# One power for both norms of a mixing layer, its squares summed on the scalar engine, and its plain rows written later

## The chip, the core and the metric

The kernel runs on one core of a Trainium2 chip. A core has five engines that each work through a queue of their own, in order, and wait for each other by semaphores: TensorE (PE, matrix products and transposes; PEld is its weight load), VectorE (DVE), ScalarE (ACT), GpSimd (POOL, which also issues the gathers), and SyncE (SP, which here only issues plain DMAs). The metric is the device time of one execution in microseconds (us), the median of a few runs.

## The reference

The input is eight sequences (batches) of 512 rows with 128 features. Six layers follow one another, each added to the rows: a mixture of experts, attention, the same experts again, a layer whose operands are rounded to six bits (fp6), the mixing layer with a gated feed-forward, and the fp6 layer once more. The change lies in the fifth. With x the normalised input of that layer, n its layer norm:

```python
def _layernorm(x): return (x - mean(x)) / sqrt(var(x) + 1e-5)
def _rmsnorm(x, w): return x * rsqrt(mean(x * x) + 1e-6) * w

n = _layernorm(x)                       # the rows that the layer takes
xn = _rmsnorm(n, rms_mix_w)
g, v, d = xn @ Wg.T + bg, xn @ Wv.T + bv, xn @ Wd.T + bd
h = scan(h * (0.001 + 0.998 * sigmoid(d)) + sigmoid(g) * tanh(v))   # along the sequence
u = n + h
xf = _rmsnorm(u, rms_ffn_w)
y = u + (silu(xf @ W_gate.T) * (xf @ W_up.T)) @ W_out.T
x = x + y
```

The layer therefore needs two norms of the same input, n and xn, then a third of u. All norms go over the 128 features of a row.

## The kernel before, in words

A batch is held in SBUF as `X[b]`, 128 partitions by 4 tiles of 128 features, so a row lies in one partition and a batch's statistics are 128 by 4 numbers. Everything stays in SBUF from the first layer to the last, except the rows that are sorted to experts through DRAM.

**Tails.** The last three layers of a batch, from the first fp6 layer to the store, are its tail: `tail(b)` runs `fp6(b, 3)`, `mix(b)`, `fp6(b, 5)` and then issues the store on SP. A tail starts when both experts' outputs of its batch have been gathered (POOL's indirect DMAs, tile `y`) and added (`x<-y,g,x` on DVE). Eight tails run, and at most four at a time: `flight = Slots(4)` in line 1392. A tail that finds no slot waits until another has stored. Smaller counters do the same for parts: `rounding`, `turning`, `gating` and `feeding`, two each (line 1275).

**Order.** The instruction order on each engine is that of the program (`tc.manual_schedule()`), and the program's order is made by a planner, the class `Clock`. Each tail is a Python generator; a `yield` ends one step. `finish` takes the generator that is ready first by the planner's own rough costs (`took`) and lets it issue its next step on whatever engines that step names. So a `yield` is a place where steps of other tails, of the experts' tiles or of a gather can come between; without it, the instructions stand back to back in their queues. Because a queue is in order, an instruction that waits also holds back everything behind it, whoever's it is.

**The norms.** `moments` makes mean and variance by bn_stats and bn_aggr on DVE. `power` (line 401) adds an epsilon on DVE and raises to -1/2 on POOL, 128 by 4 numbers. `normed_act` (line 419) makes the shift -mean/sigma on DVE and then scales and shifts the four tiles on ACT, with scale and bias read per partition.

**mix before.** Its first part is a chain over the engines: moments (DVE, tiles `st_m`, `mv_m`), epsilon (DVE) and power (POOL, `rs_m`), two products that give the mean square of n (DVE, `r`), the shift (DVE, `nb_um_m`), the plain rows u (ACT, `um_m`), a second epsilon (DVE) and power (POOL) in `rs_ma`, its product with `rs_m` (DVE), a second shift (DVE, `nb_row_m`), and the rows xn (ACT, `row_m`). Then PE transposes xn (`tp_xn`), ACT copies it out with the weight (`uT_xn`), PE makes three products (`pgd`, `pgg`, `pgv`), and ACT takes their tanh (`gtd`, `gtg`, `gtv`). DVE maps the decay to 0.499 d + 0.5 (`gtd`), makes the scan's input (`gtg`) and scans (`scan`), PE turns the result back (`tp_h`), and DVE adds it to u (`um_m<-tp_h,um_m`).

Its second part is the feed-forward. Moments of u (DVE, `st_f`, `mv_f`), mean squared plus variance (two on DVE, `r2f`), epsilon (DVE) and power (POOL, `rs_mb`), `X[b] + u` (POOL), u scaled (ACT, `xf`), transposed and copied, six products (`gt`, `up`), silu on ACT and a product on DVE for each of three pairs, twelve products into `yo`, and the addition to X.

Tiles come from pools with a fixed number of buffers per tag: `um` has 4 (u of the mixing layer and of the fp6 layers), and `row` has 4 (xn, the scan's output, xf).

Of the kernel before, what the change touches and what calls it, by code (L numbers as in the profile page):

```python
# [9 lines left out]
F32 = mybir.dt.float32  # L10
BF16 = mybir.dt.bfloat16
I32 = mybir.dt.int32
AF = mybir.ActivationFunctionType
ALU = mybir.AluOpType
# [3 lines left out]
P = 128  # L18
S = 512
NT = S // P  # L20
# [214 lines left out]
def kernel(  # L235
# [18 lines left out]
    ck = Clock(nc)  # L254
    nb = x.shape[1] // S
    assert nb == 8
    scale = 1.0 / float(DK) ** 0.5
# [3 lines left out]
    wk = ctx.enter_context(tc.tile_pool(name="wk", bufs=2))  # L261
    small = ctx.enter_context(tc.tile_pool(name="small", bufs=5))
# [5 lines left out]
    X = []  # L268
# [29 lines left out]
    mhalf = cpool.tile([P, GTX], F32, tag="mhalf", name="mhalf")  # L298
# [87 lines left out]
    def bank(name):  # L386
        return p_ps.tile([P, S], F32, tag="ps", name=name)
# [5 lines left out]
    def turned(src, name):  # L393

        tp = bank(f"tp_{name}")
        for t in range(NT):
            ck.tensor.transpose(tp[:, ts(t, P)], src[:, t, :], ident)
        return tp


    def power(v, eps, name):
        rs = small.tile([P, NT], F32, tag="rs", name=f"rs_{name}")
        ck.vector.tensor_scalar_add(rs, v, eps)
        yield
        ck.gpsimd.tensor_tensor(rs, rs, mhalf[:, 0:NT], ALU.pow)
        yield
        return rs

    def moments(src, name, mv=None):
        st = small.tile([P, NT, ck.vector.BN_STATS_DIM], F32, tag="bst", name=f"st_{name}")  # L410
        if mv is None:
            mv = small.tile([P, NT, ck.vector.BN_AGGR_DIM], F32, tag="bmv", name=f"mv_{name}")
        for t in range(NT):
            ck.vector.bn_stats(out=st[:, t, :], in_=src[:, t, :])
        for t in range(NT):
            ck.vector.bn_aggr(out=mv[:, t, :], in_=st[:, t, :])
        return mv

    def normed_act(src, mv, rs, name, tag="u"):

        nb_ = small.tile([P, NT], F32, tag="nbias", name=f"nb_{tag}_{name}")
        ck.vector.scalar_tensor_tensor(nb_, mv[:, :, 0], -1.0, rs, ALU.mult, ALU.mult)
        yield
        u = wk.tile([P, NT, P], F32, tag=tag, name=f"{tag}_{name}", bufs={"um": 4, "row": 4}.get(tag, 2))
        for t in range(NT):
            ck.scalar.activation(
                u[:, t, :], src[:, t, :], AF.Identity,
                scale=rs[:, t : t + 1], bias=nb_[:, t : t + 1],
            )
        yield "product"  # L430
        return u
# [11 lines left out]
    def by_feature(src, name, scale=None, tag="uT"):  # L443

        tp = turned(src, name)
        yield
        ut = wk.tile([P, S], F32, tag=tag, name=f"uT_{name}")
        if scale is None:
            ck.scalar.copy(ut, tp)
        else:  # L450
            ck.scalar.activation(ut, tp, AF.Copy, scale=scale)
        yield "product"
        return ut
# [850 lines left out]
    def vec(i):  # L1304
        return vec_s[:, i : i + 1]

    def mix(b):
        mv = moments(X[b], f"m_{b}")
        rs = yield from power(mv[:, :, 1], 1e-5, f"m_{b}")

        r2 = small.tile([P, NT], F32, tag="r2", name=f"r2_{b}")
        ck.vector.tensor_tensor(r2, rs, rs, ALU.mult)
        ck.vector.tensor_tensor(r2, r2, mv[:, :, 1], ALU.mult)
        u = yield from normed_act(X[b], mv, rs, f"m_{b}", tag="um")
        rr = yield from power(r2, 1e-6, f"ma_{b}")
        ck.vector.tensor_tensor(rr, rr, rs, ALU.mult)
        xn = yield from normed_act(X[b], mv, rr, f"m_{b}", tag="row")
        yield from turning.take()
        xnt = yield from by_feature(xn, f"xn_{b}", scale=vec(V_MIX))
        yield from gating.take()  # L1320

        def gate(i, bias, half, n):
            pg = bank(f"pg{n}_{b}")
            ck.tensor.matmul(pg, wmix_s[:, ts(i, P)], xnt, start=True, stop=True)
            t = wk.tile([P, S], F32, tag=("qm", "ka", "qa")[i], name=f"gt{n}_{b}", bufs=(2, KBUFS, 2)[i])
            ck.scalar.activation(t, pg, AF.Tanh, bias=bias, scale=half)
            return t


        d = gate(2, half_vec[:, 1:2], 0.5, "d")  # L1330
        g = gate(0, half_vec[:, 0:1], 0.5, "g")
        vv = gate(1, vec(V_BV), 1.0, "v")
        turning.give()
        yield
        ck.vector.tensor_scalar(d, d, 0.499, 0.5, ALU.mult, ALU.add)
        ck.vector.scalar_tensor_tensor(g, g, 1.0, vv, ALU.add, ALU.mult)
        h = wk.tile([P, NT, P], F32, tag="row", name=f"scan_{b}", bufs=4)
        ck.vector.tensor_tensor_scan(
            h.rearrange("p t d -> p (t d)"), d, g, 0.0, ALU.mult, ALU.add
        )  # L1340
        gating.give()
        yield
        ht = turned(h, f"h_{b}")
        yield
        uf = u.rearrange("p t d -> p (t d)")
        ck.vector.scalar_tensor_tensor(uf, ht, 0.5, uf, ALU.mult, ALU.add)
        mv = moments(u, f"f_{b}")
        r2 = small.tile([P, NT], F32, tag="r2", name=f"r2f_{b}")
        ck.vector.tensor_tensor(r2, mv[:, :, 0], mv[:, :, 0], ALU.mult)
        ck.vector.tensor_tensor(r2, r2, mv[:, :, 1], ALU.add)  # L1350
        rr = yield from power(r2, 1e-6, f"mb_{b}")
        ck.gpsimd.tensor_tensor(X[b], X[b], u, ALU.add)
        xf = wk.tile([P, NT, P], F32, tag="row", name=f"xf_{b}", bufs=4)
        for t in range(NT):
            ck.scalar.activation(xf[:, t, :], u[:, t, :], AF.Copy, scale=rr[:, t : t + 1])
        yield
        yield from feeding.take()
        xft = yield from by_feature(xf, f"xf_{b}", scale=vec(V_FFN), tag="u")
        yield from gating.take()
        sgs = []  # L1360
        for f in range(NGF):
            pg, pu = bank(f"gt_{b}_{f}"), bank(f"up_{b}_{f}")
            ck.tensor.matmul(pg, wmix_s[:, ts(3 + f, P)], xft, start=True, stop=True)
            ck.tensor.matmul(pu, wmix_s[:, ts(6 + f, P)], xft, start=True, stop=True)
            sg = wk.tile([P, S], F32, tag=("qm", "ka", "qa")[f], name=f"silu_{b}_{f}", bufs=(2, KBUFS, 2)[f])
            ck.scalar.activation(sg, pg, AF.Silu)
            yield
            ck.vector.tensor_tensor(sg, sg, pu, ALU.mult)
            sgs.append(sg)
            yield  # L1370
        yo = bank(f"yo_{b}")
        for t in range(NT):
            for f in range(NGF):
                ck.tensor.matmul(
                    yo[:, ts(t, P)], sgs[f][:, ts(t, P)], wout_s[:, f, :],
                    start=(f == 0), stop=(f == NGF - 1),
                )
        gating.give()
        feeding.give()
        yield  # L1380
        xb = X[b].rearrange("p t d -> p (t d)")
        ck.vector.tensor_tensor(xb, xb, yo, ALU.add)

    def tail(b):
        yield from fp6(b, 3)
        yield from mix(b)
        yield from fp6(b, 5)
        nc.sync.dma_start(
            out=out[:, ts(b, S)].rearrange("p (t d) -> p t d", t=NT), in_=X[b]
        )  # L1390
# [130 lines left out]
```

## Time and profile before

| | |
|---|---|
| median of 3 runs | 1151.93 us (1150.66 to 1154.56) |
| the profiled execution, its own time | 1150.87 us |
| its span, first to last instruction | 1149.2 us |
| mean granted TensorE clock | 0.923 |
| busy over the span | PE 960.0, DVE 706.1, POOL 544.8, ACT 483.4 us |
| instructions | 20659 |
| first and last start of a tail's first bn_stats (tile `st`, late part) | 844 us, 1055.20 us |

All instructions show line 185, that of a helper which records every operation for the planner, so they are told apart by tile names. Times inside a row of the timeline are counted from the start of the span. A row's name is output<-inputs, with numbers of buffers and batches left out. In a list of waits, "A <- B" is idle time of A's engine that ended with B. A table of groups gives how often an instruction ran, its total and its mean duration. Many short DVE operations overlap a little with their neighbours, so a sum of durations is slightly more than the time that they fill.

### The profile page before, as it was taken

The numbers are of one execution on the slowest core, as the hardware profiler recorded it, in microseconds if no ns is written. First come the engines' busy times: TensorE is split into PE (matmuls) and PEld (weight loads), VectorE is DVE, ScalarE is ACT, GpSimd is POOL, SyncE is SP. The second block draws the span as 40 slices with busy tenths as digits, with TensorE's granted clock in tenths as the row PEclk, the third lists the DMA queues.
The fourth block names the chain that finished last, engine by engine and source line by source line (L and its number), as shares of the span: only waits on it lengthen the run. The fifth ranks groups of instructions, "written<-read, shape, count | busy, mean of one in ns | idle before, by whom it ended". The sixth has DMA issues, their size and how long they took to land.

```text
span 1149.2 us, 20659 instructions
## 1 busy us (share of the span) xinstructions
PE 960.0 (84%) x6705; PEld 662.2 (58%) x6705; DVE 706.1 (61%) x2636; ACT 483.4 (42%) x1063; POOL 544.8 (47%) x694
## 2 busy tenths in 40 slices
PE   3569999999998989999997999998089985765773
PEld 2469999776444444444545767767077764433542
DVE  7323345466878877767795655314256786888764
ACT  1323333325554545455554544543034544344531
POOL 3777071213876845454552231231745646864422
PEclk9999999999998988989999999999589998887786
DMA  9579788756900100000014444342366401100000
GB/s 294 192 248 277 234 263 255 212 177 173 284 22 26 32 12 8 13 9 13 8 33 140 123 136 121 118 141 61 116 201 189 142 20 37 31 25 10 1 19 18
DMA packets 122363, 127.33 MB, mean 111 GB/s; under 512 B 9616, under 2 KB 103696, under 8 KB 122256
## 3 DMA queue, kind: packets, MB, share of 16 engines
q1 hardware_dynamic: 114064, 109.22, 31.5%
q0 software_dynamic: 8192, 16.79, 4.6%
q8 instruction: 53, 0.87, 0.3%
q14 instruction: 54, 0.44, 0.1%
HBM read 79.58 MB, written 46.40 MB: 110 GB/s over the span
## 4 chain that ended last, share of the span: by engine, by line
PE 63%; DVE 19%; POOL 6%; issue 5%; ACT 3%; DMA 2%; SPq 1%; POOLq 0%; DVEq 0%; ACTq 0%
PE yp L185 14%; PE hp L185 14%; PE sa L185 10%; PE av L185 6%; PE sb L185 4%; DVE seen L185 2%; DVE q L185 2%; DVE x L185 2%; POOL y L185 2%; PE xp L185 2%; DVE st L185 1%; PE lp L185 1%; PE yo L185 1%; ACT um L185 1%; PE tp L185 1%
## 5 line engine op out<-in xcount | busy, mean ns | idle before, releaser
L185 DVE CUSTOM_DVE_ANT_0 seen<-sa,future_s 128x128 f32<-128x128 f32 (+3 forms) x512 | 224.7, 487 | 92.5 <-PE sb L185 74.9
L185 ACT ACTIVATE pm<-sb 128x512 f32<-128x512 f32 (+1 forms) x384 | 182.1, 524 | 201.0 <-PE sb L185 188.0
L185 ACT ACTIVATE hs<-hp,wx 128x256 f32<-128x256 f32 x276 | 120.6, 471 | 265.7 <-PE hp L185 236.5
L185 PE MATMUL sb<-qa,ka 32*128 32x512 f32 (+3 forms) x1024 | 224.4, 480 | 8.8 <-DVE nstat L185 6.8
L185 POOL TENSOR_SCALAR_AFFINE_SELECT pm<-pm 128x256 f32<-128x256 f32 x256 | 101.1, 409 | 223.0 <-ACT pm L185 219.9
L185 PE MATMUL sa<-ka,qz 32*128 32x256 f32 (+3 forms) x1024 | 200.6, 477 | 1.6 <-issue 1.6
L185 PE MATMUL yp<-wx,hs 128*128 128x128 f32 x1472 | 198.7, 278 | 2.5 <-DVE hs L185 2.0
L185 PE MATMUL hp<-xt,wx 128*128 128x256 f32 x736 | 198.6, 395 | 0.0
L185 PEld LDWEIGHTS yp<-wx,hs 128*128 128x128 f32 x1472 | 188.8, 194 | 13.0 <-issue 5.2
L185 POOL DMA_INDIRECT y<-rows_out,at x128 | 136.1, 1064 | 85.6 <-DMA rows_out<-yo 41.8
L185 DVE TENSOR_SCALAR hs<-hp,wx 128x256 f32<-128x256 f32 x92 | 44.3, 481 | 175.6 <-ACT hs L185 157.1
L185 PEld LDWEIGHTS hp<-xt,wx 128*128 128x128 f32 x736 | 131.4, 197 | 27.3 <-issue 10.2
L185 PEld LDWEIGHTS sa<-ka,qz 32*128 32x128 f32 x1024 | 96.6, 190 | 61.8 <-issue 19.6
L185 PEld LDWEIGHTS sb<-qa,ka 32*128 32x128 f32 x1024 | 106.0, 189 | 26.8 <-DVE nstat L185 14.2
L185 PE MATMUL av<-pm,vpad 128*32 128x512 f32 (+3 forms) x1024 | 92.1, 455 | 0.0
L185 POOL TENSOR_TENSOR rs<-rs,mhalf 128x4 f32<-128x4 f32 (+1 forms) x36 | 39.7, 1104 | 97.6 <-DVE rs L185 94.7
L185 PE MATMUL xp<-cst,xs 128*128 128x128 f32 x184 | 37.9, 290 | 51.7 <-DMA xs<-by_stretch 38.4
L185 POOL DMA_INDIRECT by_stretch<-um,sat x64 | 64.4, 1007 | 18.5 <-issue 14.4
L185 PEld LDWEIGHTS xp<-cst,xs 128*128 128x128 f32 x184 | 26.4, 149 | 63.2 <-issue 51.5
L185 PEld LDWEIGHTS av<-pm,vpad 128*32 128x32 f32 x1024 | 23.6, 109 | 66.2 <-issue 42.3
L185 DVE COPY xt<-xp 128x256 f32<-128x256 f32 x92 | 38.2, 415 | 37.3 <-PE xp L185 37.2
L185 DVE SCALAR_TENSOR_TENSOR x<-y,g,x 128x128 f32<-128x128 f32 x128 | 55.8, 439 | 3.6 <-DMA y<-rows_out,at 1.3
(219 smaller groups left out, 1332.8 us busy)
## 6 DMA issues: line engine op xcount, KB each, us to landing
wx<-in_wexp SPq DMA_DIRECT2D x92, 578.0 KB, 4.0
rows_out<-yo SPq DMA_DIRECT2D x92, 128.0 KB, 1.8
by_stretch<-zero SPq DMA_DIRECT2D x8, 1280.0 KB
rows_in<-zero SPq DMA_DIRECT2D x2, 3456.0 KB
by_stretch<-zero SPq DMA_DIRECT2D x8, 768.0 KB, 11.9
xs<-rows_in SPq DMA_DIRECT2D x46, 128.0 KB, 4.4
xs<-by_stretch SPq DMA_DIRECT2D x46, 128.0 KB, 3.4
x<-in_x SPq DMA_DIRECT2D x8, 256.0 KB, 5.4
```

Source lines behind the costliest of these rows:

```text
L185: return call(*args, **kw)
```

## The change

In `mix` both powers are taken together. Since the mean square of n is v/(v + 1e-5) for variance v, the second norm's factor is the power -1/2 of v(1 + 1e-6) + 1e-6 * 1e-5. One tile `rs2` of 128 by 2 by 4 gets both arguments (two DVE operations), one POOL power and one DVE operation for both shifts (`nb2`). The rows xn are made directly after; the plain rows u are made on ACT after the gates. The map of the decay to 0.499 d + 0.5 goes from DVE to ACT. In the feed-forward the moments of u and the two operations on them go; ACT squares the four tiles of u with a sum along the row into `r2` (its output is the buffer of xf, which is written over afterwards), and one DVE operation scales by 1/128 and adds the epsilon. Further `yield`s stand between these steps. No DMA, no matrix product and no buffer count changes.

```diff
     def mix(b):
         mv = moments(X[b], f"m_{b}")
-        rs = yield from power(mv[:, :, 1], 1e-5, f"m_{b}")
-
-        r2 = small.tile([P, NT], F32, tag="r2", name=f"r2_{b}")
-        ck.vector.tensor_tensor(r2, rs, rs, ALU.mult)
-        ck.vector.tensor_tensor(r2, r2, mv[:, :, 1], ALU.mult)
-        u = yield from normed_act(X[b], mv, rs, f"m_{b}", tag="um")
-        rr = yield from power(r2, 1e-6, f"ma_{b}")
-        ck.vector.tensor_tensor(rr, rr, rs, ALU.mult)
-        xn = yield from normed_act(X[b], mv, rr, f"m_{b}", tag="row")
+        rs2 = small.tile([P, 2, NT], F32, tag="rs2", name=f"rs2_{b}")
+        ck.vector.tensor_scalar(
+            rs2[:, 1], mv[:, :, 1], 1.0 + 1e-6, 1e-6 * 1e-5, ALU.mult, ALU.add
+        )
+        ck.vector.tensor_scalar_add(rs2[:, 0], mv[:, :, 1], 1e-5)
+        yield
+        ck.gpsimd.tensor_tensor(
+            rs2, rs2, mhalf[:, 0 : 2 * NT].rearrange("p (k t) -> p k t", k=2), ALU.pow
+        )
+        yield
+        nb2 = small.tile([P, 2, NT], F32, tag="nb2", name=f"nb2_{b}")
+        ck.vector.scalar_tensor_tensor(
+            nb2, mv[:, :, 0].unsqueeze(1).to_broadcast([P, 2, NT]), -1.0, rs2, ALU.mult, ALU.mult
+        )
+        yield
+        xn = wk.tile([P, NT, P], F32, tag="row", name=f"xn_{b}", bufs=4)
+        u = wk.tile([P, NT, P], F32, tag="um", name=f"um_m_{b}", bufs=4)
+
+        def scaled(dst, k, lo, hi):
+            for t in range(lo, hi):
+                ck.scalar.activation(
+                    dst[:, t, :], X[b][:, t, :], AF.Identity,
+                    scale=rs2[:, k, t : t + 1], bias=nb2[:, k, t : t + 1],
+                )
+
+        scaled(xn, 1, 0, NT)
+        yield "product"
         yield from turning.take()
         xnt = yield from by_feature(xn, f"xn_{b}", scale=vec(V_MIX))
         yield from gating.take()
...
         g = gate(0, half_vec[:, 0:1], 0.5, "g")
         vv = gate(1, vec(V_BV), 1.0, "v")
         turning.give()
-        yield
-        ck.vector.tensor_scalar(d, d, 0.499, 0.5, ALU.mult, ALU.add)
+        ck.scalar.activation(d, d, AF.Copy, scale=0.499, bias=0.5)
+        scaled(u, 0, 0, NT)
+        yield
         ck.vector.scalar_tensor_tensor(g, g, 1.0, vv, ALU.add, ALU.mult)
...
         ck.vector.scalar_tensor_tensor(uf, ht, 0.5, uf, ALU.mult, ALU.add)
-        mv = moments(u, f"f_{b}")
+        yield
+
+        xf = wk.tile([P, NT, P], F32, tag="row", name=f"xf_{b}", bufs=4)
         r2 = small.tile([P, NT], F32, tag="r2", name=f"r2f_{b}")
-        ck.vector.tensor_tensor(r2, mv[:, :, 0], mv[:, :, 0], ALU.mult)
-        ck.vector.tensor_tensor(r2, r2, mv[:, :, 1], ALU.add)
-        rr = yield from power(r2, 1e-6, f"mb_{b}")
+        for t in range(NT):
+            ck.scalar.activation(
+                xf[:, t, :], u[:, t, :], AF.Square, accum_out=r2[:, t : t + 1]
+            )
+        yield
+        rr = small.tile([P, NT], F32, tag="rs", name=f"rs_mb_{b}")
+        ck.vector.tensor_scalar(rr, r2, 1.0 / P, 1e-6, ALU.mult, ALU.add)
+        yield
+        ck.gpsimd.tensor_tensor(rr, rr, mhalf[:, 0:NT], ALU.pow)
         ck.gpsimd.tensor_tensor(X[b], X[b], u, ALU.add)
-        xf = wk.tile([P, NT, P], F32, tag="row", name=f"xf_{b}", bufs=4)
+        yield
         for t in range(NT):
             ck.scalar.activation(xf[:, t, :], u[:, t, :], AF.Copy, scale=rr[:, t : t + 1])
         yield
```

## The prediction

> **What bounds the kernel now.** I read the busy time by stage first, then the engines' timelines over the last stage, then the list of waits there, and last the groups of instructions for durations. Times are us from the start of the span. First, busy time of each engine in three stretches: the first tails beside the last expert tiles, then the second set of gathers, then the end.
>
> ```profile
> core 0: us, PE busy (x) PEld busy (x) DVE busy (x) ACT busy (x) POOL busy (x), PEclk, DMA share, GB/s
> 845.00:960.00 115.00, 101.68 (x591) 83.51 (x590) 82.61 (x258) 56.50 (x126) 60.98 (x55) 0.96 0.39 118
> 960.00:1055.00 95.00, 57.05 (x222) 36.62 (x221) 76.35 (x225) 39.71 (x88) 67.32 (x61) 0.77 0.09 25
> 1055.00:1149.00 94.00, 61.76 (x255) 41.99 (x253) 61.24 (x180) 34.97 (x76) 32.72 (x30) 0.78 0.04 14
> ```
>
> See in the last two rows that no engine is full: DVE is at 80% and 65%, PE at 60% and 66%, ACT at 42% and 37%. Everything changed lies after 844, where the tails begin, so the 844 us before are untouched. What sets the end after 960 is latency, the time that one tail needs from engine to engine, with DVE's queue as the main delay. Next, DVE's timeline where the last tail starts, and where its mixing layer begins and waits:
>
> ```profile
> 1054.62 0.67 DVE L185 SCALAR_TENSOR_TENSOR x<-yp,x 128x512 f32<-128x512 f32 x1
> 1055.20 0.86 DVE L185 BATCH_NORM_STATS2 st<-x 128x6 f32<-128x128 f32 x4
> ...
> 1075.72 0.87 DVE L185 BATCH_NORM_STATS2 st_m<-x 128x6 f32<-128x128 f32 x4
> ...
> 1086.49 0.16 DVE L185 TENSOR_SCALAR rs_ma<-r 128x4 f32<-128x4 f32 x1
> ...
> 1089.83 0.19 DVE L185 SCALAR_TENSOR_TENSOR nb_row_m<-mv_m,rs_ma 128x4 f32<-128x4 f32 x1
> ```
>
> The first line is the last addition of another tail. The eighth tail starts right behind it, although its rows have been complete since about 1034, when the last `x<-y,g,x` ends: it waited for one of the four slots. The tail that held that slot started at 924 (`st` at 923.91). So two tails in series, 924 to 1055 (131 us) and 1055 to 1149 (94 us), set the end, and what a tail gains there counts twice, until the rows' own 1034 becomes the limit. Then the chain inside the last mixing layer, on ACT and on POOL:
>
> ```profile
> 1080.81 1.65 ACT L185 ACTIVATE um_m<-x,nb_um_m,rs_m 128x128 f32<-128x128 f32 x4
> ...
> 1090.06 1.65 ACT L185 ACTIVATE row_m<-x,nb_row_m,rs_ma 128x128 f32<-128x128 f32 x4 [4.36 <-DVE nb_row_m L185]
> ```
>
> ```profile
> 1077.16 1.01 POOL L185 TENSOR_TENSOR rs_m<-rs_m,mhalf 128x4 f32<-128x4 f32 x1 [4.32 <-DVE rs_m L185]
> ...
> 1086.73 1.02 POOL L185 TENSOR_TENSOR rs_ma<-rs_ma,mhalf 128x4 f32<-128x4 f32 x1 [2.54 <-DVE rs_ma L185]
> ```
>
> The power itself is 1 us; nearly all of the 9.25 us between the two ACT rows is the second trip through queues. The list of waits after 840 agrees; idle us in total, times, longest:
>
> ```profile
> ACT row_m L185 <- DVE nb_row_m L185: 24.8, 8, 6.5
> ...
> POOL rs_ma L185 <- DVE rs_ma L185: 14.2, 5, 4.8
> ```
>
> **What the Trainium skill says.** *ScalarE: Activation LUTs*, section "What ACT_TABLE_LOAD costs": an ACTIVATE with immediates takes 186 ns + 0.833 ns per element, each per-partition operand adds 93 ns, and neighbours overlap by about 93 ns. The trace agrees: 128 elements with two such operands give 479 by the page and 480 as the median of `um`; with one, 386 and 387 (`xf`). *ScalarE activation tables: per-element evaluation and per-set limits*, section "What a function is on this engine": the same operands cost the same whatever function, and the accumulator output works with any; what reading it out costs isn't given, nor shown here. *SBUF — State Buffer*, section "Who interferes with whom": some DVE operations and POOL exclude each other on a shared port. The trace fits: `rs_ma`'s 128x4 addition has a median of 162 ns and a maximum of 1232, when POOL was busy.
>
> **The change, part by part.** Durations are from the groups after 840, for all eight tails:
>
> ```profile
> L185 POOL TENSOR_TENSOR rs_ma<-rs_ma,mhalf 128x4 f32<-128x4 f32 x8 | 8.7, 1082 | 14.3 <-DVE rs_ma L185 14.2
> L185 POOL TENSOR_TENSOR rs_m<-rs_m,mhalf 128x4 f32<-128x4 f32 x8 | 8.5, 1062 | 15.4 <-DVE rs_m L185 11.6 <-DVE nb_um L185 3.8
> ...
> L185 DVE BATCH_NORM_STATS2 st_f<-um_m 128x6 f32<-128x128 f32 x32 | 7.0, 281 | 0.3
> ...
> L185 DVE TENSOR_SCALAR gtd<-gtd 128x512 f32<-128x512 f32 x8 | 3.4, 428 | 3.2 <-ACT gtd L185 3.2
> ```
>
> *One power, xn first.* From the start of `st_m` to the start of `row_m` the eight mixing layers take 13.8, 16.9, 16.9, 19.0, 15.5, 19.6, 11.4 and 14.3 us, mean 15.9; to the start of `um_m` 4.8, 7.5, 7.3, 9.8, 6.4, 11.0, 4.3 and 5.1, mean 7.0. The second is the very chain that will lead to xn: moments, epsilon, power, shift, ACT. Added to it are one more DVE operation of 0.17 (as `rs<-mv`, 172 ns) and a power over 8 columns in place of 4. The only other width shown is 20 columns, 3.53 us against 1.04 for 4, so 0.156 us a column and 1.65 for 8 (bounds 1.04, no cost for width, and 2.1, double). Thus 7.0 + 0.2 + 0.6 = 7.8 and a saving of **8.1 us** a tail, of which queueing is the larger part. Bounds: 2.5, the second trip of two powers and a few short operations if nothing queued, and 11.
>
> *Plain rows behind the gates.* ACT's four `um_m`, 1.65 us, are moved, not added. They and the decay's map follow `gtv`. The map costs 186 + 0.833 x 512 = 613 ns by the page (an estimate; `uT_xd`'s copy of this size takes 581); DVE loses 0.43. The scan needs both the map (0.6 after `gtv`) and `gtg` (0.69 after `gtv`), so the map is hidden under `gtg`. The rows are ready 2.3 us after `gtv`; the addition of `tp_h` comes no sooner than 0.69 + 1.22 (scan) + 1.09 (`tp_h`) = 3.0. Cost on the path 0; without that cover at most 2.3. But whatever stands behind them in ACT's queue, such as a `uT_xd` for which PE waits, can be held by 2.3 us; before, it was held by the same 1.65 earlier.
>
> *Squares on ACT.* From `um_m<-tp_h` to `xf` before: 8.1, 4.0, 4.7, 4.4, 5.8, 5.0, 4.4 and 3.6, mean 5.0. The last one meets next to no other work: 0.69 addition, 1.62 moments and products, then epsilon and a 1.02 power. DVE's 1.62 go. Four squares take 4 x 293 less overlaps, 0.9 us by the page (an estimate), with the price of one read-out unknown: bounds 0.9 and 2.4 (0.39 as `xf` has, plus 0.2 for each read-out, both taken high); I take 1.5. So the bare chain is even, but there are two more hand-overs, DVE to ACT and back, each with a `yield` before the next. The two hand-overs of before cost (5.0 - 3.6) / 2 = 0.7 each, the three of the first chain about (7.0 - 2.9) / 3 = 1.4, with 2.9 its bare sum. Two at 1.0 give **-2.0 us** a tail (bounds 0 and -4). The square waits at ACT's head for the addition on DVE; behind it stand other tails' copies and gates, for which PE waits.
>
> *Load.* DVE loses `st_f` 7.0, `mv_f` 2.9, `r2f` 3.1, both `r` 4.3, `rs_ma` 2.3 and 1.9, one shift 1.3 and `gtd` 3.4, in all 26.2, and gains 1.4: 24.8 us for eight, 3.1 a tail. Of DVE's 138 us after 960 about 15 go. ACT gains some 2.1 a tail, 17 for eight on 131 of 304 us: 49% busy, no bound. POOL loses 17.2 and gains 13.2. PE, SP and every DMA keep their work. Buffers: xf takes its `row` buffer a few us sooner, but one tail never holds two at once and four may fly, so 4 suffice; no wait is priced.
>
> *Sum.* A tail gains 8.1 - 2.0 = 6.1, two in series 12.2. For DVE work of the other tails that is out of the way I add 1.3, little, since the means above already hold the queue. 13.5 off the profiled span of 1149.2 gives 1135.7; the profiled execution's own time was 1.7 above its span, so 1137.4, and the median of the runs is 1.1 above that execution: **1138 us**. The eighth tail would start near 1049, still behind the 1034 of its rows.
>
> **The rivals.** *More (B).* DVE's queue is what the tails wait for, and 15 us less of it shortens every hand-over. The fourth and the eighth mixing layer then save 9 and 10.5 as their own rows allow, with 6 us from the fp6 layers beside them: 26 us, 1126. For it: DVE at 80%. Against it: PE's `yo` runs of 4.6 to 4.8 us in the end, which nothing shortens.
>
> *Hidden (C).* The gates come earlier but find PE or the two `turning` and `gating` slots taken, and the tail ends where it ended; within 3 us, about 1151. For it: PE at 14.7 of 15 us in 1065 to 1080. Against it: PE is at two thirds over the stage.
>
> *Slower (D).* The squares hold ACT. The planner books them as if the addition came on time, but DVE runs late, by up to 6.5 us where `row_m` waited. If every square waits so, ACT holds the `uT_xd`, gates and silus of three other tails each time. It decides when the hold costs the two serial tails more than the 8.1 each gained: at 10 each, +4, 1156. A table reload would add to it: the page names relu, copy, identity and abs as in every set, not Square; two loads of 1.28 a tail would leave 3.5 of the 6.1. Against it: ACT is idle for more than half of the stage. The same end comes if the new order puts a tail behind gathers that wait on POOL, as one did at 959 (5.1 us).
>
> **How the numbers follow.** The forecast has 0.60 with 1128 to 1146; B 0.20, C 0.08, D 0.12. A difference of 0.3%, 3.5 us, is about what a measurement of this kernel can tell from no change. The forecast and B are faster by more, 0.80; C is the same, 0.08; D slower, 0.12. The range goes from 1122, which leaves out the far end of B, to 1150, which leaves out D and a part of C; the order that the planner will make can't be read from this trace, and that is most of its width.
>
> **What would show it.** Right: from `st_m` to `row_m` about 8 us in place of 15.9; DVE about 25 us lower, ACT about 17 higher; the POOL power over 8 columns near 1.65; `um_m<-tp_h` to `xf` near 7; the last tail's start near 1049, and some 88 us from there to the end. Wrong: rows of xn that still start 12 us or more after `st_m`, ACT waits of several us at the squares ended by DVE's addition, table loads beside them, or a last tail that starts at 1055 as before.

## The result and the profile after

The changed kernel takes **1140.76 us** in the median of four runs (1139.76 to 1142.06) against 1151.65 for the kernel before beside it (1150.66 to 1154.56): a ratio of 0.9904, with a 95% interval of 0.9881 to 0.9927. That is 10.9 us less where 13.5 were forecast. The profiled execution took 1139.76 us, its span is 1138.0, so 11.2 shorter than before. First the page's busy times of the changed kernel.

```profile
span 1138.0 us, 20611 instructions
PE 953.5 (84%) x6705; PEld 659.0 (58%) x6705; DVE 684.6 (60%) x2516; ACT 496.1 (44%) x1135; POOL 539.0 (47%) x686
```

DVE has 21.5 us less than before, ACT 12.7 more, POOL 5.8 less. Next, the busy time by stage, cut as it was for the kernel before: start and length of the stretch, busy us of each engine, granted clock, DMA share, GB/s.

```profile
core 0: us, PE busy (x) PEld busy (x) DVE busy (x) ACT busy (x) POOL busy (x), PEclk, DMA share, GB/s
845.00:960.00 115.00, 102.32 (x607) 84.31 (x606) 78.98 (x235) 63.70 (x161) 62.68 (x56) 0.96 0.38 115
960.00:1055.00 95.00, 57.66 (x238) 39.74 (x237) 71.49 (x190) 43.60 (x106) 62.37 (x55) 0.80 0.10 31
1055.00:1138.00 83.00, 52.53 (x223) 34.37 (x221) 47.87 (x116) 36.47 (x97) 30.64 (x26) 0.77 0.03 13
```

Still no engine is full after 960; DVE is at 75% and 58% in the last two rows. The end is still latency, and the third row is the shorter one. Now the two rows that answer to the start of the last tail: DVE's timeline of the changed kernel (start, us, engine, line, operation, output<-input).

```profile
1045.73 1.46 DVE L185 SCALAR_TENSOR_TENSOR x<-y,g,x 128x128 f32<-128x128 f32 x2
1047.11 0.86 DVE L185 BATCH_NORM_STATS2 st<-x 128x6 f32<-128x128 f32 x4
```

Before, `st` of the last tail stood directly behind `x<-yp,x`, the last addition of the tail that gave up its slot. Now it stands directly behind `x<-y,g,x`, the last addition of its own rows. The slot had come free earlier: the fourth tail's last `x<-yp,x` in the same timeline is this.

```profile
1032.23 0.69 DVE L185 SCALAR_TENSOR_TENSOR x<-yp,x 128x512 f32<-128x512 f32 x1 [0.87 <-PE yp L185]
```

So the slot was free at 1032.9 (before: 1055.3), and the rows were complete only at 1047.2. Before, they were complete at 1034.2, with this row of DVE's timeline:

```profile
1033.54 0.71 DVE L185 SCALAR_TENSOR_TENSOR x<-y,g,x 128x128 f32<-128x128 f32 x2
```

**What holds the last tail has changed.** It isn't the only one: the sixth and the seventh tail wait for their rows too. They start at 1010.5 and 1039.4, though slots were free from 987.2 and 1016.6 on; before, they started at 997.2 and 1027.2, within 2 us of the slots at 995.4 and 1027.3. Here are, after the change, the third tail's last addition, then the seventh tail's rows and start:

```profile
1015.87 0.69 DVE L185 SCALAR_TENSOR_TENSOR x<-yp,x 128x512 f32<-128x512 f32 x1 [2.06 <-PE yp L185]
...
1038.70 0.73 DVE L185 SCALAR_TENSOR_TENSOR x<-y,g,x 128x128 f32<-128x128 f32 x2
1039.35 0.86 DVE L185 BATCH_NORM_STATS2 st<-x 128x6 f32<-128x128 f32 x4
```

Why the rows are late is in POOL's timeline. Here are the first and the last gather of the last three batches, before, then after.

```profile
959.15 1.09 POOL L185 DMA_INDIRECT y<-rows_out,at  x1 [5.13 <-issue]
...
1025.55 1.07 POOL L185 DMA_INDIRECT y<-rows_out,at  x1 [0.18 <-issue]
```

```profile
970.79 1.09 POOL L185 DMA_INDIRECT y<-rows_out,at  x1 [6.63 <-DMA rows_out<-yo]
...
1041.96 1.07 POOL L185 DMA_INDIRECT y<-rows_out,at  x1 [0.18 <-issue]
```

After the change the first of these gathers comes 11.6 us later and waits on POOL for the experts' last store. The 24 gathers then take 71 us instead of 66. The store is late because of PE's order. In PE's timeline `hp` is an expert tile's first product, and `yo` from `wout_s` is the end of a tail's feed-forward (24 records a tail). Before, then after:

```profile
935.48 2.50 PE L185 MATMUL yo<-wout_s,silu 128*128 128x128 f32 x20 [1.37 <-DVE silu L185]
...
944.98 1.03 PE L185 MATMUL hp<-xt,wx 128*128 128x256 f32 x4
955.94 0.61 PE L185 MATMUL yo<-wout_s,silu 128*128 128x128 f32 x4
```

```profile
926.31 2.50 PE L185 MATMUL yo<-wout_s,silu 128*128 128x128 f32 x20 [1.08 <-DVE silu L185]
...
952.75 1.03 PE L185 MATMUL hp<-xt,wx 128*128 128x256 f32 x4
953.61 3.05 PE L185 MATMUL yo<-wout_s,silu 128*128 128x128 f32 x24
959.15 1.03 PE L185 MATMUL hp<-xt,wx 128*128 128x256 f32 x4
```

Before, one feed-forward ran ahead of the last expert tile; now two do, and with it more of the tails' other products and transposes: that tile's first product comes 14.2 us later (959.15 against 944.98), of which the second `yo` itself is 3. The first tails became shorter, the planner therefore put more of them ahead of the experts' last work, and this delays the rows of the last three batches.

In eight of the twelve runs below the first 200 us moved 180 to 184 GB/s in place of 250 to 252, the tails begin some 60 to 70 us later, and the kernel before takes 1214 to 1218 us beside them, so only ratios are compared between these runs and the others.

### The profile page after: what moved, and what is told of

It reads as the page before. It is cut to its first block, busy times and chain, and to the rows that moved or that the text cites. A ratio compares the mean times of both kernels' runs of the same rounds, so it can differ in the third digit from the quotient of the medians.

```text
span 1138.0 us, 20611 instructions
## 1 busy us (share of the span) xinstructions
PE 953.5 (84%) x6705; PEld 659.0 (58%) x6705; DVE 684.6 (60%) x2516; ACT 496.1 (44%) x1135; POOL 539.0 (47%) x686
## 4 chain that ended last, share of the span: by engine, by line
PE 66%; DVE 16%; POOL 5%; issue 5%; ACT 5%; DMA 2%; SPq 1%; POOLq 0%; DVEq 0%; ACTq 0%
PE yp L185 15%; PE hp L185 14%; PE sa L185 10%; PE av L185 6%; PE sb L185 4%; DVE seen L185 2%; DVE q L185 2%; DVE x L185 2%; PE yo L185 2%; PE xp L185 2%; POOL y L185 1%; PE lp L185 1%; DVE st L185 1%; PE tp L185 1%; ACT um L185 1%
## 5 line engine op out<-in xcount | busy, mean ns | idle before, releaser
L185 POOL DMA_INDIRECT y<-rows_out,at x128 | 132.7, 1037 | 88.0 <-DMA rows_out<-yo 48.3
L185 PEld LDWEIGHTS sa<-ka,qz 32*128 32x128 f32 x1024 | 96.7, 190 | 61.7 <-issue 20.2
L185 POOL TENSOR_TENSOR rs<-rs,mhalf 128x4 f32<-128x4 f32 (+2 forms) x44 | 53.6, 1219 | 109.8 <-DVE rs L185 97.7
```

Of the source, the lines that this page charges most:

```text
L185: return call(*args, **kw)
```

## The experiments

Each profile was read for two times: when the slot is free (the last addition of the fourth tail), and when the last rows are complete (the last `x<-y,g,x`). Theory 1 is the prediction's, that tails in series set the end; Theory 2 is that after the change the last rows do.

The first four and the last four runs have the later beginning. No profile of the kernel before with that beginning was kept, so where a stretch of theirs is set against the kernel before, that is its profile with the earlier one.

**The first part alone.** The one power with xn first; u made directly after xn, the map on DVE and the moments of u kept:

```diff
...
+        scaled(xn, 1, 0, NT)
+        scaled(u, 0, 0, NT)
+        yield "product"
...
```

> The kernel before with the one power alone: xn is made from it at once, the plain rows u directly behind xn on the scalar engine; the decay's map stays on DVE and the feed-forward keeps its moments of u. Theory 1 (the tails' own chain in series sets the end, as in the prediction): from st_m to xn about 4.4 us in place of 15.9 as in the changed kernel, and nothing lost behind the addition of tp_h; two tails in series give 15 to 23 us, so 1129 to 1137 us, faster than the whole change. Theory 2 (after the change the end is set by the rows of the last three batches, which come later because the first four tails push the last expert tiles back): the last expert store again comes some 10 us later than before, the last tail starts when its rows are complete, and the end is within 5 us of the whole change, 1136 to 1146 us.

Measured: 1225.83 us against 1214.43, ratio 1.0081 (1.0057 to 1.0104). The xn rows do come early: 6.1 us after `st_m`, mean of eight. But the way from xn to the addition of `tp_h` is 20.2 us (18.7 in the profile of the kernel before) and from `xf` to the end of the mixing layer 31.4 (28.0). That u, now in ACT's queue ahead of what PE waits for, is a part of it is argued. The slot is free only at 1132.1 and the last tail starts there. Both theories had forecast a gain; a shorter stretch inside a tail didn't give a shorter kernel.

**The squares alone.** The kernel before with the feed-forward's part of the change.

```diff
-        mv = moments(u, f"f_{b}")
+        yield
...
+        for t in range(NT):
+            ck.scalar.activation(
+                xf[:, t, :], u[:, t, :], AF.Square, accum_out=r2[:, t : t + 1]
+            )
+        yield
...
```

> The kernel before with the squares on the scalar engine alone, with their yields; both powers stay. Theory 1: from the addition of tp_h to xf about 10 us in place of 5.0, so two tails in series lose 5 to 11 us, less some 2 to 4 for the lighter DVE: 1153 to 1161 us. Theory 2: the first four tails become slower, the experts finish at the time of before or sooner, and the loss shows only in the last tail: 1150 to 1156 us.

Measured: 1199.82 us, ratio 0.9875 (0.9836 to 0.9915), against my expectation. Its own stretch did become longer, as expected: 8.8 us from the addition of `tp_h` to `xf`. Yet a mixing layer from `st_m` to `x<-x,yo` takes 61.0 us, where power_only's takes 62.2 and that of the kernel before took 67.7 in its profile. The gain lies in the stretches that were not edited: 15.5 from xn to the addition (18.7 before), 23.4 from `xf` to the end (28.0 before). The program order differs, and I put the gain down to it, but that, and which step of the order brings it, is only argued.

**Without the squares.** The change with the old feed-forward norm.

```diff
+        mv = moments(u, f"f_{b}")
...
+        rr = yield from power(r2, 1e-6, f"mb_{b}")
...
-        for t in range(NT):
-            ck.scalar.activation(
-                xf[:, t, :], u[:, t, :], AF.Square, accum_out=r2[:, t : t + 1]
-            )
...
```

> The changed kernel with the feed-forward's moments of u put back on DVE (power, late plain rows and the map on ACT stay). Theory 1: from the addition of tp_h to xf 5 us again in place of 10.4, which is 5 us a tail and 10 in series, less 2 to 4 for DVE's 1.9 us more a tail: 1132 to 1136 us. Theory 2: the first four tails get still faster and push the experts back further, the last tail (whose own time from that addition to xf was 3.6 us with the squares too) gains nothing: 1138 to 1146 us.

Measured: 1216.52 us, ratio 1.001 (0.9989 to 1.003): no gain. The mixing layer is the shortest of all, 56.0 us, and the last tail starts at 1124.56. The slot was free at 1112.4; the rows were complete at 1124.6. Two feed-forwards stand ahead of the last expert tile's first product here, and a third ahead of its second. The wait is that of Theory 2: 12 us of what the tails gained were waited away. The ratio is above what either theory had forecast.

**Fewer places to change over.** The change without three `yield`s between addition, squares, epsilon and `xf`.

```diff
         ck.vector.scalar_tensor_tensor(uf, ht, 0.5, uf, ALU.mult, ALU.add)
-        yield
...
-        yield
         rr = small.tile([P, NT], F32, tag="rs", name=f"rs_mb_{b}")
...
         ck.gpsimd.tensor_tensor(X[b], X[b], u, ALU.add)
-        yield
```

> The changed kernel without three of the new yields: the squares follow the addition of tp_h in the same step, the epsilon operation the squares, and the scaling of xf the addition to X. The same instructions in another order. Theory 1: the waits between the steps go, from the addition to xf 6 us in place of 10.4, so about 8 us in series: 1131 to 1135 us. Theory 2: within 4 us of the change, 1137 to 1145 us. A third reading, that the planner's order as such moves the time by some us whichever way: anything outside both, with the time of the last tail and the start of it moved without relation to that interval.

Measured: 1218.18 us, ratio 1.0023 (1.0005 to 1.004). From the addition to `xf` it takes 5.0 us, where the change takes 10.4 in its own profile: the hand-overs, not the squares, are the price. The kernel doesn't gain by it; the ratio is outside both forecasts. Two rows of DVE's timeline of this run say why: the last tail stands behind its own rows again, and its slot had been free since 1114.7.

```profile
1126.64 1.42 DVE L185 SCALAR_TENSOR_TENSOR x<-y,g,x 128x128 f32<-128x128 f32 x2
1127.98 0.86 DVE L185 BATCH_NORM_STATS2 st<-x 128x6 f32<-128x128 f32 x4
```

**The rows earlier, in both kernels.** These four ran together, with the earlier beginning of the result. The change was run once more as a base:

> The whole change, unaltered, beside its parts: the chip of the first four experiments ran the stretch before the tails some 65 us longer, kernel before included, so ratios to the kernel before on the same chip are compared from here on. Both theories: 0.990 as in the result (0.985 to 0.995). If the ratio lies near 1.00, where the change without the squares (1.001) and the change with fewer yields (1.002) lie, then what those two lost is the chip's and not theirs.

Measured: 1140.55 us against 1151.05, ratio 0.9904 (0.9882 to 0.9925); rows complete at 1047.5, last tail from 1047.46. Then one edit that lets a tile's two gathers of the last group stand back to back, in the changed kernel and in the kernel before. No work is added or taken away.

```diff
     def moe_combine(s, g):
...
-                    yield
+                    if (s, g) != (2, 1) or k == 1:
+                        yield
```

> The changed kernel, with the two gathers of a tile of the last three batches issued in one step of the planner (no yield between them), so that they stand closer together in POOL's queue. Experts and the first tails keep their order. Theory 2: the 24 gathers take 55 us or less in place of 71, the last tail starts 10 us sooner, ratio 0.980 to 0.986. Theory 1: within 3 us of the change, 0.988 to 0.993.

> The same packing in the kernel before, where the last tail waited for a slot until 1055 while its rows were complete at 1034. The gathers come sooner, but the slot is what the last tail waits for: 0.996 to 1.003 by both theories. If it gains as much as the packed change does (0.99 or less), the rows were what set the end in the kernel before as well, and my reading of the slot is wrong.

Measured, in the changed kernel: 1134.26 us, ratio 0.9859 (0.983 to 0.9888). The gathers take 60 us in place of 71 (55 were expected), the rows are complete at 1037.6, and the last tail starts 6.7 us sooner. The timeline of DVE shows it behind a slot again, at 1040.76:

```profile
1040.15 0.69 DVE L185 SCALAR_TENSOR_TENSOR x<-yp,x 128x512 f32<-128x512 f32 x1
1040.76 0.86 DVE L185 BATCH_NORM_STATS2 st<-x 128x6 f32<-128x128 f32 x4
```

In the kernel before: 1152.72 us, ratio 1.0007 (0.9995 to 1.0018). There the rows come 10 us earlier too (1024.1 against 1034.2), but the slot is free at 1061.2, and nothing is won:

```profile
1060.47 0.68 DVE L185 SCALAR_TENSOR_TENSOR x<-yp,x 128x512 f32<-128x512 f32 x1
1061.07 0.86 DVE L185 BATCH_NORM_STATS2 st<-x 128x6 f32<-128x128 f32 x4
```

This profile is of the longest of the twelve executions (1156.59 us), whose tails begin 5.4 us later than in the profile of the kernel before; counted from there, the rows come 15.6 us earlier and the slot 0.4 later. The same edit gains 6.3 us in the one kernel and nothing in the other. **This pair decides for Theory 2 in the changed kernel and for Theory 1 in the kernel before.** In the changed kernel the gain stops where the slot becomes the limit: it came free 7.3 us later than without the edit (1040.8 against 1033.5). Why is argued: the gathers stand closer together on POOL, and the sixth and seventh tails, which start 5.6 and 12.4 us sooner, share the engines with the fourth.

**Expert tiles first.** Once a tail holds one of the four slots (`flight.n` counts the free ones), the planner prefers the experts' tiles by 1 us.

```diff
-            g = min(live, key=lambda g: max(self.ready.get(g, 0.0), now))
+            ahead = 1.0 if self.early() else 0.0
+            g = min(
+                live, key=lambda g: max(self.ready.get(g, 0.0), now) - ahead * (g in self.flowing)
+            )
...
+    ck.early = lambda: flight.n < 4
```

> The changed kernel with one term in the planner: once a tail has started, the stream of expert tiles counts as ready 1 us sooner than it is. The instructions are the same; in PE's queue 8 transposes and no down-projection of the feed-forward (yo) of the tails stand before the last expert product, in the changed kernel 43 transposes and 24 yo, in the kernel before 28 and 12. Theory 1 (the tails in series set the end): the first tails are held back by the experts, the end comes later than the change's, ratio 0.993 to 1.005. Theory 2 (the rows of the last three batches set it): last expert store some 10 us sooner in relation to the first tail's start, first gather behind it sooner by as much, ratio 0.978 to 0.988.

Measured: 1138.1 us, ratio 0.9885 (0.9863 to 0.9906), 2.5 us below `change_again`, just above what Theory 2 had forecast. In PE's timeline the last expert product now comes ahead of all feed-forwards:

```profile
922.70 1.03 PE L189 MATMUL hp<-xt,wx 128*128 128x256 f32 x4
938.54 1.06 PE L189 MATMUL yo<-wout_s,silu 128*128 128x128 f32 x4
```

The first gather follows at 933.65, 38 us earlier than in `change_again`, and the rows are complete at 1013.5, 34 us earlier. But the first tails pay: their slot is free at 1051.6, and the last tail starts at 1051.54. DVE:

```profile
1050.94 0.69 DVE L189 SCALAR_TENSOR_TENSOR x<-yp,x 128x512 f32<-128x512 f32 x1
1051.54 0.86 DVE L189 BATCH_NORM_STATS2 st<-x 128x6 f32<-128x128 f32 x4
```

So the two limits are two ends of one balance, and one can be bought with the other.

**Both orders,** packed gathers and a preference of 0.5 us, and the three parts once more beside it:

> The changed kernel with both edits of order: the gathers of the last three batches packed in pairs, and the expert tiles counted ready 0.5 us sooner once a tail has started (in PE's queue 12 yo before the last expert product, in the changed kernel 24). By the reading so far the last tail starts at the later of two times, the end of the fourth tail and the completion of the last rows, and then needs 83 to 92 us. With 1 us of preference the slot was the later one (1051.6), with the packing alone the two stood at 1041 and 1038. In between, the fourth tail should end at 1036 to 1044 with rows before 1030: span 1124 to 1134 us, ratio 0.978 to 0.986. If the end does not follow the later of the two, the reading falls.

> The one power alone again, since its first run was on the chip with the longer beginning (ratio 1.008 there, where the fourth tail's end at 1132.1 set the start of the last). In PE's queue 12 yo stand before the last expert product, as in the kernel before, so the experts are not pushed back; the fourth tail gains some 8 to 11 us in its mixing layer. Reading of the two limits: slot at about 1045, rows near 1034, ratio 0.988 to 0.994. If the ratio is again 1.008, the one power without the lighter feed-forward is a loss by itself.

> The squares alone again, for the same reason (ratio 0.9875 on the other chip, where I had expected a loss). 12 yo before the last expert product. If the squares are a loss of 5 us in each of two serial tails, as the whole change's trace suggests from the addition of tp_h to xf, the ratio is 1.000 to 1.008; if DVE's lighter queue, 1.9 us a tail, gives more than the two hand-overs cost, it is 0.985 to 0.995 here too.

> The change without the squares again (ratio 1.001 on the other chip, where the rows set the last start). 36 yo stand before the last expert product in place of 24, so the rows are complete later than in the change by 5 us or more, 1052 or later, and the last tail starts with them: ratio 0.993 to 1.000. If it is 0.986 or less, the squares cost time in the change and what I call the rows' limit does not hold.

Measured with the later beginning: both orders 1204.26 us against 1218.38, ratio 0.9869 (0.9824 to 0.9913); the power alone 1.0091 (1.0059 to 1.0123), the squares alone 0.9897 (0.9855 to 0.9939), without squares 0.999 (0.9974 to 1.0007). The parts repeat: the power alone is no gain a second time, against my forecast, and the squares alone are one. With both orders the ratio just misses the forecast; the rows are complete at 1080.7, 32 us ahead of the slot at 1112.3, which was too much of a good thing: some of the first tails' time was given away for rows that then waited.

The reading by two limits, over the profiles of this study that show a different kernel or a different limit (us):

| kernel | slot free | rows complete | last tail starts | span |
|---|---|---|---|---|
| before | 1055.3 | 1034.2 | 1055.20 | 1149.2 |
| before_packed | 1061.2 | 1024.1 | 1061.07 | 1154.9 |
| the change | 1032.9 | 1047.2 | 1047.11 | 1138.0 |
| change_packed | 1040.8 | 1037.6 | 1040.76 | 1132.6 |
| change_experts_first | 1051.6 | 1013.5 | 1051.54 | 1134.4 |
| power_only | 1132.1 | 1126.2 | 1131.99 | 1224.5 |
| squares_only | 1108.0 | 1103.2 | 1107.96 | 1197.6 |
| no_squares | 1112.4 | 1124.6 | 1124.56 | 1216.4 |
| few_yields | 1114.7 | 1128.1 | 1127.98 | 1216.4 |
| change_both_orders | 1112.3 | 1080.7 | 1112.25 | 1205.6 |

The last tail starts at the later of the two everywhere, within 0.15 us. (The `st` of the last tail may overlap the end of the instruction before it, so it starts a little ahead.)

## Why the prediction was right, and where it was not

The direction and the size held: 1138 forecast (its own sum gives 1138.5), 1140.76 measured, within the range. But the sum came out near for partly wrong reasons: one term was too small, one too large, and the limit wasn't the one named.

**One power, xn first: right, and under-sized.** From `st_m` to the first xn row it takes 4.4 us in the mean, not 7.8: 11.5 saved, not 8.1. I had kept the hand-overs at the 1.4 each that the old chain showed. They all but vanished, to (4.4 - 3.7) / 3 = 0.2, where 3.7 is the old bare 2.9 with the 0.2 and 0.6 that were added. (The durations in the groups of the kernel before add up to 2.7 for the bare chain, not 2.9; with that it is 0.3.) The last tail, on POOL and then on ACT, shows the chain nearly bare:

```profile
1070.44 1.65 POOL L185 TENSOR_TENSOR rs<-rs,mhalf 128x8 f32<-128x8 f32 x1 [0.18 <-DVE rs L185]
```

```profile
1072.33 1.65 ACT L185 ACTIVATE xn<-x,nb,rs 128x128 f32<-128x128 f32 x4 [1.67 <-DVE nb L185]
```

The power over 8 columns has 1.65 here and a mean of 1.72 over eight, as estimated from the widths 4 and 20.

**Squares on ACT: the operation was sized well, the hand-overs were not.** These groups of the changed kernel after 840 give total and mean ns:

```profile
L185 ACT ACTIVATE xf<-um_m 128x128 f32<-128x128 f32 x32 | 9.5, 299 | 9.4 <-DVE um_m L185 9.4
L185 ACT ACTIVATION_READ_ACCUMULATOR xf<-um_m 128x1 f32 x32 | 6.0, 189 | 0.0
L185 ACT ACT_TABLE_LOAD x1 | 1.3, 1283 | 0.0
```

A square is 299 ns, where the Trainium skill, *ScalarE: Activation LUTs*, section "What ACT_TABLE_LOAD costs", gives 186 + 0.833 x 128 = 293. Four with their read-outs fill 1.3 us (1.5 forecast). In the last tail the whole stretch from the addition to `xf` is 3.6 us (1089.74 to 1093.32), as it was before: the bare chain is even, as said. But the mean went from 5.0 to 10.4, a loss of 5.4 where I took 2.0 and bounded it at 4.0. Not the wait that I feared at ACT's head is what costs: that is 9.4 us for all eight together, 3.5 the longest. The loss comes behind the squares. The first tail, all engines: addition at 885.27, squares from 886.05 to 887.33, and then

```profile
890.86 0.48 DVE L185 TENSOR_SCALAR hs<-hp,wx 128x256 f32<-128x256 f32 x1 [4.91 <-ACT hs L185]
...
893.64 0.16 DVE L185 TENSOR_SCALAR rs_mb<-r2f 128x4 f32<-128x4 f32 x1
893.82 1.77 POOL L185 TENSOR_TENSOR rs<-rs,mhalf 128x8 f32<-128x8 f32 x1 [5.08 <-DVE rs_mb L185]
895.58 1.00 POOL L185 TENSOR_TENSOR rs_mb<-rs_mb,mhalf 128x4 f32<-128x4 f32 x1
...
899.44 1.26 ACT L185 ACTIVATE xf<-um_m,rs_mb 128x128 f32<-128x128 f32 x4
```

The epsilon, 0.16 us of work, starts 6.3 us behind the squares. For 3.5 of these DVE does nothing: an experts' `hs` stands ahead of the epsilon in its queue and waits for ACT. The rest is that tile's and another tail's work. The power then stands behind another tail's power on POOL, and `xf` behind other work of ACT. A `yield` at each hand-over lets others in each time. few_yields, with 5.0 in this stretch, confirms it.

**Rows behind the gates: right, no cost.** From xn to the addition of `tp_h` it went from 18.7 to 16.7 us. The rows are hidden, and the map takes 620 ns for 613 estimated. power_only, where u stands ahead of the gates, shows 20.2 for the same stretch, though in a run with the later beginning.

**The sum of a tail.** A mixing layer from `st_m` to `x<-x,yo` went from 67.7 to 57.3 us, 10.4 saved for 6.1 forecast: 11.5 from `st_m` to xn, 2.0 to the addition of `tp_h`, 5.4 lost to `xf`, and 2.3 behind it (28.0 to 25.7), where nothing was edited and nothing was forecast. So rival C, that the earlier gates gain nothing, didn't come.

**Two tails in series: the step that failed.** The prediction let the gain count twice "until the rows' own 1034 becomes the limit", and held that the eighth tail would start "still behind the 1034 of its rows". It treated 1034 as fixed. The slot was freed 22.4 us earlier, not 6.1, since the fourth tail took 112 us for 131 and began 3.4 sooner. Of its 19, 14.5 lie in its mixing layer and 6.6 in its last fp6 layer, with 2.2 lost in its first. The late rows may have a part in the 6.6, as they left the engines to fewer tails; this is argued. But the faster first tails went ahead of the last expert tile, and the rows moved to 1047.2. So 8.1 of the 22.4 became an earlier start. That it starts near 1049 as forecast is two errors that cancel. The last tail then gained 3.1 us (94.0 to 90.9), half of the 6.1 forecast: its mixing layer gained 6.2, while its first fp6 layer took 21.6 for 20.5 and its last 19.1 for 17.0. It now starts 7.8 us behind the seventh tail (28 before) and shares the engines with it. That this closeness costs it is argued: change_experts_first, with 25.7 us between them, has a last tail of 82.9, but change_both_orders, with 24.2, has one of 93.3. 8.1 + 3.1 = 11.2, the whole of what the span lost.

**Load and rivals.** DVE lost 21.5 of 24.8, ACT gained 12.7 of 17, POOL lost 5.8 for 4: right in kind. Rival D named two mechanisms. The table reload didn't come: one load stands in this stage, as before. The other did come, in small: "the new order puts a tail behind gathers" (the one at 970.79 waits 6.6 us on POOL, and `q` of two tails stands behind it). Rival B has its fourth tail right and more than right (mixing layer 70.0 to 55.5), but its rows don't allow it.

**What stays open.** With the later beginning the whole change wasn't run in its own order, so what it gives there is unknown, and its 0.990 can't be set against the parts, all run there: those with one power don't gain, the squares alone do. Why they do is open: the order is one reading, DVE's lighter queue (1.9 us a tail, by the second forecast) another, and no run parts the two. A fifth slot in flight wasn't tried.

## What to carry to other kernels

Where work is put in order by what is ready first, a faster step doesn't only end earlier: it takes a place in the queues ahead of other work, and the time of that other work isn't a constant. So for each limit that "lies well ahead", ask what sets it and whether the edit can move it. Count hand-overs rather than instructions: moving 1.6 us of work to an idle engine was even by itself and cost 5.4 us in queues; and before shortening a tail further, look at which instruction stands directly in front of its first one. Here the version with the gathers packed, 1134.26 us, is the fastest of those that ran together, 6.3 us below the change.

## What the hardware showed that was not expected

- An ACTIVATE with a sum along the row is followed by an instruction of its own, ACTIVATION_READ_ACCUMULATOR, 189 ns for 128 by 1; it overlaps its neighbours, and so squares follow one another every 290 to 310 ns.
- The first 200 us, which no edit here touches, moved 250 to 252 GB/s in some runs and 180 to 184 in others, and the tails then stood some 60 to 70 us later. The granted TensorE clock of this stretch was 1.00 in the former and 0.89 to 0.90 in the latter; which of the two brings the other, or what brings both, is open.
